# Context turned in two groups of 64 partitions in an adaLN cross-attention block (one core of Trainium2)

## The chip, the core and the metric

The kernel runs on one core of one Trainium2 chip. Its engines are TensorE (PE; PEld is its weight load), VectorE (DVE), ScalarE (ACT), GpSimd (POOL) and SyncE (SP), each with an instruction queue of its own that it works through in order. The metric is the device time of one launch in microseconds, lower being better. All numbers are float32 except a few bfloat16 helpers.

## The reference

One transformer block with modulation, for 16 batches of 224 tokens of width 512, 16 heads of 32, and a context of 750 rows per batch:

```python
x_norm = modulate(_ln(x), shift_a, scale_a)
q, k, v = split(x_norm @ W_qkv + b_qkv)             # self-attention
x = x + gate_a * (softmax(q k^T * scale) v @ W_proj + b_proj)
q_c = _ln(x) @ W_qc + b_qc                           # cross-attention
k_c, v_c = split(_ln(context) @ W_kvc + b_kvc)
x = x + (softmax(q_c k_c^T * scale) v_c @ W_cproj + b_cproj)
h = gelu(modulate(_ln(x), shift_m, scale_m) @ W_mlp1 + b_mlp1) @ W_mlp2 + b_mlp2
x = x + gate_m * h
```

The change touches only how `_ln(context)` is brought into the form that `k_c` and `v_c` are computed from.

## The kernel before

The kernel runs in three stages: self-attention (to about 727 us of the profiled execution), cross-attention (to about 2190 us), and the MLP. Nearly every instruction is issued through the `Ordered` helper (line 28 in the profile), so each engine's order is the program's order. Which tile waits for which is worked out from the tiles; a pool gives out its buffers in turn, and a tile waits until the readers of the tile that had the buffer before are done.

**Units.** Cross-attention runs over 64 units (b, g), batch b and group g of four heads (line 1093). A unit computes its scores in three parts n = 0, 1, 2, each of two chunks of 125 context rows; a part fills the four banks of `ps_s`, of which there is one set, so part n + 1 waits until part n has been read by `keep`: on VectorE into the running maximum `top`, and on ScalarE into the tile `pt`. After each part two slots of other work run: slots 0 and 1 after part 0, 2 and 3 after part 1, 4 and 5 after part 2. Between them lie the steps of the unit before: `subtract(0)` and `weights(0)` between slots 0 and 1, `subtract(1)` between slots 2 and 3, `weights(1)` after slot 3. `subtract` spreads the maxima on PE (`o<-ident,mc`) and adds them on VectorE; `weights` takes three exponentials on ScalarE and sums them on GpSimd. The unit ends with `maxima`, which turns `top` on PE into two banks. It turns rows 0 to 63 into one bank and rows 64 to 124 into the other, as two instructions of 64 and 61 rows. The next unit begins with the value products of the unit two before.

**The plan.** `at_slot(b, g, slot, f)` (lines 919 to 976) appends work to a slot; what is appended first runs first. What matters here, for batch b from 1 on, n = b + 1:

- slots 0 and 1 of every unit: `project_k` of the next unit's keys, halves 0 and 1 of the context (PE, then ScalarE empties the bank into `kt`);
- slots 2 and 4 of unit (b, 0): `project_v` of chunks 4 and 5 of batch b; slots 2 and 4 of (b, 2): of chunks 1 and 2 of batch n (PE, then ScalarE copies the bank into `vt`);
- slot 3 of (b, 0) and of (b, 2): the context of batch n is turned, half 0 and half 1, three chunks each (`turn_ctx`), and then the loads of batch b + 2 are issued on SP (`load_ctx`);
- slot 5 of these units: `project_q` (PE, then ScalarE into `qt`).

In batch 0, half 0 of the next batch is turned in slot 5 of (0, 0), the values of chunks 0 to 3 take other slots, and slot 0 of (0, 2) holds a product for a bias (`make_bcproj`). Before the first unit a prologue turns both halves of batch 0. Batch 15 turns nothing.

**PSUM.** All eight banks are in use: four for scores (`ps_s`), one for outputs (`ps_o`, line 235), and three in `ps_mm` (line 234: `name="at_mm", bufs=3`), from which `project_k`, `project_v`, `project_q`, `turn_ctx` and `maxima` take a bank each, and `maxima` two.

**Turning.** The context chunk `cx[b, c]` is a normalised tile of 125 rows on partitions and 512 columns. `turn_ctx(b, c)` turns its four blocks of 125 x 128 into one bank of 128 x 500, and ScalarE copies the bank into the half's tile `cxt` (128 partitions, 4 blocks, 375 rows). The chunk is the weight operand, a unit matrix of 125 x 125 is what streams.

## Time and profile before

| | |
|---|---|
| median of 3 runs | 2915.72 us (2912.17 to 2917.97) |
| the profiled execution: device time | 2912.48 us |
| its span, first to last instruction | 2910.7 us |
| mean granted TensorE clock | 0.993 |
| busy share of the span: PE, DVE, POOL, ACT | 97%, 66%, 43%, 38% |
| cross-attention, 742 to 2190 us: PE, DVE, POOL, ACT busy | 1416, 1132, 926, 829 us of 1448 |
| turns of `cx`: instructions, PE busy | 384, 46.7 us |
| copies of turned context on ScalarE: instructions, busy | 96, 49.3 us |

A line of a group has the source line, the engine, the operation, the tile written and those read, the shape and the count, then busy time and mean nanoseconds of one, then the engine's idle time before the group and what ended most of it. A line of a timeline has the start, the time from the first start to the last end of the merged instructions, engine, operation, and in brackets the idle time before. A line of the chain of waits has the start, the time that the chain spent there, and the engine and tile. One matrix product of float32 shows as two MATMUL records, a turn as one. PE's instructions overlap: a product or turn starts before the last one has ended, so the step from start to start is what a stream of them costs.

### The profile page before, as it was taken

How to read it: one execution, taken by the hardware profiler on the slowest of the kernel's cores; microseconds unless marked ns; L12 is line 12 of the kernel's file. 1: busy time of each engine (PE TensorE's matmuls, PEld its weight loads, DVE VectorE, ACT ScalarE, POOL GpSimd, SP SyncE). 2: the span in 40 equal slices, each digit the busy share in tenths (PEclk: the TensorE clock that was granted, in tenths of full speed). 3: DMA queues.
4: the chain of work that ended last, by engine and by line, in shares of the span. 5: the costliest groups of instructions: out<-in, count | busy, mean ns of one | idle time of the engine just before them, and what ended most of it. 6: DMA issues, size and time to landing. Idle time of an engine off the chain costs nothing.

```text
span 2910.7 us, 46976 instructions
## 1 busy us (share of the span) xinstructions
PE 2833.8 (97%) x19693; PEld 1809.3 (62%) x19693; DVE 1929.8 (66%) x2752; ACT 1119.6 (38%) x1402; POOL 1241.7 (43%) x1379
## 2 busy tenths in 40 slices
PE   8999999998999999999999999999978999999999
PEld 3444444444555565655655655666545888888888
DVE  4666776676478778787787787787785543444343
ACT  1222222221456655665565556656543112112211
POOL 1022222122357666676666666666654410221021
PEclk9999999999999999999999999999989999999999
DMA  6111110100100010100001100100013111110110
GB/s 191 59 33 33 32 33 10 60 11 29 52 32 24 22 35 24 35 32 21 29 25 34 35 24 23 34 25 24 22 44 107 55 37 37 44 57 29 46 44 29
DMA packets 55385, 114.44 MB, mean 39 GB/s; under 512 B 4309, under 2 KB 4373, under 8 KB 55173
## 3 DMA queue, kind: packets, MB, share of 16 engines
q1 hardware_dynamic: 54560, 110.58, 11.8%
q8 instruction: 155, 2.54, 0.4%
q10 hardware_dynamic: 612, 0.85, 0.1%
q14 instruction: 58, 0.47, 0.1%
HBM read 89.33 MB, written 22.09 MB: 38 GB/s over the span
## 4 chain that ended last, share of the span: by engine, by line
PE 79%; DVE 10%; ACT 5%; issue 4%; POOL 2%; DMA 1%; SPq 0%; POOLq 0%; ACTq 0%; DVEq 0%
PE mm L28 43%; PE a L28 10%; PE sc L28 10%; PE o L28 8%; PE b L28 5%; ACT pt L28 4%; DVE at L28 3%; PE c L28 3%; DVE top L28 2%; POOL acc L28 1%; DVE stats L28 1%; DVE m L28 1%; DVE mc L28 1%; ACT kt L28 1%; DMA gate<-gate_d 1%
## 5 line engine op out<-in xcount | busy, mean ns | idle before, releaser
L28 POOL TENSOR_TENSOR acc<-acc,pt 125x448 f32<-125x448 f32 x512 | 584.4, 1141 | 40.2
L28 ACT COPY pt<-sc 125x1792 f32<-125x1792 f32 x192 | 317.3, 1653 | 563.0 <-DVE top L28 509.9
L28 DVE TENSOR_TENSOR pt<-pt,o 125x896 f32<-125x896 f32 x384 | 394.2, 1081 | 87.0 <-PE o L28 84.6
L28 DVE TENSOR_TENSOR top<-top,sc 125x896 f32<-125x896 f32 x320 | 346.6, 1083 | 35.4 <-PE sc L28 28.7
L28 PE MATMUL mm<-wkvc,cxt 128*125 128x512 f32 x768 | 354.4, 604 | 6.9 <-ACT kt L28 6.9
L28 PE MATMUL mm<-cxt,wkvc 128*128 128x375 f32 x1024 | 353.3, 487 | 2.4 <-ACT cxt L28 2.4
L28 POOL TENSOR_TENSOR upd<-upd,gate 112x512 f32<-112x512 f32 (+1 forms) x60 | 78.9, 1315 | 631.7 <-DVE upd L28 627.1
L28 ACT ACTIVATE pt<-pt 125x896 f32<-125x896 f32 x384 | 338.3, 951 | 18.7 <-DVE pt L28 18.1
L28 POOL TENSOR_TENSOR acc<-pt 125x448 f32<-125x448 f32 x128 | 146.6, 1145 | 455.6 <-ACT pt L28 455.6
L28 PEld LDWEIGHTS mm<-cxt,wkvc 128*128 128x128 f32 x1024 | 184.7, 190 | 118.9 <-issue 15.4
L28 PEld LDWEIGHTS mm<-wkvc,cxt 128*125 128x125 f32 x768 | 136.4, 187 | 171.5 <-issue 153.3
L28 DVE RECIPROCAL at<-o 128x224 f32<-128x224 f32 x128 | 198.7, 1552 | 66.9 <-PE o L28 66.9
L28 ACT ACTIVATE pt<-sc 112x1792 f32<-112x1792 f32 x64 | 106.5, 1664 | 332.5 <-PE sc L28 327.9
L28 POOL TENSOR_TENSOR rstd<-mv,eps 112x2 f32<-112x2 f32 (+3 forms) x93 | 18.0, 193 | 468.7 <-DVE mv L28 468.7
L28 PE MATMUL sc<-qt,kt 32*125 32x224 f32 x3072 | 201.5, 376 | 13.9 <-ACT pt L28 13.3
L28 PE MATMUL mm<-xt,wqkv 128*128 128x448 f32 x512 | 208.6, 550 | 5.7 <-DVE xt L28 4.7
L28 DVE TENSOR_REDUCE m<-sc 112x8 f32<-112x1792 f32 x64 | 129.6, 2025 | 121.0 <-PE sc L28 121.0
L28 PEld LDWEIGHTS sc<-qt,kt 32*125 32x125 f32 x3072 | 132.9, 183 | 93.7 <-issue 33.4
L28 PE MATMUL o<-pt,vt 125*32 125x224 f32 x3072 | 158.6, 354 | 0.0
L28 PEld LDWEIGHTS mm<-xt,wqkv 128*128 128x128 f32 x512 | 92.0, 190 | 87.6 <-issue 80.4
L28 DVE TENSOR_REDUCE mc<-mm 112x8 f32<-112x512 f32 (+1 forms) x128 | 79.8, 666 | 98.4 <-PE mm L28 98.3
L28 ACT COPY mx<-a 128x512 f32<-128x512 f32 x26 | 15.2, 585 | 325.4 <-POOL upd L28 306.3
(187 smaller groups left out, 4687.2 us busy)
## 6 DMA issues: line engine op xcount, KB each, us to landing
cx<-in_ctx_dram SPq DMA_DIRECT2D x96, 250.0 KB
x<-in_x_dram SPq DMA_DIRECT2D x16, 448.0 KB
x_self<-x SPq DMA_DIRECT2D x16, 448.0 KB
x<-x_self SPq DMA_DIRECT2D x16, 448.0 KB
x_cross<-x SPq DMA_DIRECT2D x16, 448.0 KB
mx<-x_cross SPq DMA_DIRECT2D x28, 256.0 KB
w<-in_L_xcond_W_mlp_dram SPq DMA_DIRECT2D x7, 1024.0 KB
xr<-x_cross SPq DMA_DIRECT2D x28, 256.0 KB
```

The source lines that it names most:

```text
L28: return lambda *args, **kw: self.tc.keep_in_program_order(f(*args, **kw))
```

## The change

`turn_ctx` now takes a batch, a half and a list of chunks of that half. It takes two banks. Each block of a chunk is turned in two instructions, rows 0 to 63 (64 columns stream) into the first bank and rows 64 to 124 (61 columns) into the second. Chunks 0 and 1 of a half share a pair of banks; chunk 2 has a call, and a pair, of its own. ScalarE then makes one copy from each bank, in which the blocks and chunks of the bank are put in the order of `cxt`. For a half there are 24 turns where there were 12, four copies where there were three, and four banks taken where there were three.

In the plan, chunk 2 of a half goes to slot 1 of the unit, after `project_k` there, and chunks 0 and 1 to slot 3, where all three were. In batch 0, half 0 keeps slot 5 for both calls. In the prologue chunks 0 and 1 come first.

```diff
-        def turn_ctx(b, c):
-            if c % CH == 0:
-                cxt[b, c // CH] = cxt_pool.tile([P, KC, HS], F32, name="cxt")
-            ps = ps_mm.tile([P, 512], F32, name="mm")
-            for k in range(KC):
-                turn(ps[:, k * CP : (k + 1) * CP], cx[b, c][:, k * P : (k + 1) * P], ident[:CP, :CP])
-            lo = (c % CH) * CP
-            nc.scalar.copy(
-                cxt[b, c // CH][:, :, lo : lo + CP], ps[:, : KC * CP].rearrange("p (k t) -> p k t", k=KC)
-            )
+        def turn_ctx(b, hf, cs):
+
+            if (b, hf) not in cxt:
+                cxt[b, hf] = cxt_pool.tile([P, KC, HS], F32, name="cxt")
+            banks = [ps_mm.tile([P, 512], F32, name="mm") for _ in range(2)]
+            for j, c in enumerate(cs):
+                for k in range(KC):
+                    for i, (r, n) in enumerate(((0, RG), (RG, CP - RG))):
+                        lo = (j * KC + k) * n
+                        turn(
+                            banks[i][:, lo : lo + n], cx[b, hf * CH + c][r : r + n, k * P : (k + 1) * P],
+                            ident[r : r + n, r : r + n],
+                        )
+            j = len(cs)
+            dst = cxt[b, hf][:, :, cs[0] * CP : (cs[0] + j) * CP].rearrange("p k (j t) -> p k j t", j=j)
+            for i, (r, n) in enumerate(((0, RG), (RG, CP - RG))):
+                nc.scalar.copy(
+                    dst[:, :, :, r : r + n],
+                    banks[i][:, : j * KC * n].rearrange("p (j k t) -> p k j t", j=j, k=KC),
+                )
...
-                for c in range(CH):
-                    at_slot(b, 0, 3 if b else 5, lambda n=n, c=c: turn_ctx(n, c))
-                    at_slot(b, 2, 3, lambda n=n, c=c: turn_ctx(n, CH + c))
+                for cs, slot in (((2,), 1), ((0, 1), 3)):
+                    at_slot(b, 0, slot if b else 5, lambda n=n, cs=cs: turn_ctx(n, 0, cs))
+                    at_slot(b, 2, slot, lambda n=n, cs=cs: turn_ctx(n, 1, cs))
...
         for hf in range(2):
-            for c in range(hf * CH, (hf + 1) * CH):
-                turn_ctx(0, c)
+            for cs in ((0, 1), (2,)):
+                turn_ctx(0, hf, cs)
             load_ctx(1, hf)
             project_k(0, 0, hf)
```

## The prediction, made before the changed kernel ran

> **What bounds the kernel now.** I read the chain of waits first, for the engine that sets the end.

> ```profile
> PE 79%; DVE 10%; ACT 5%; issue 4%; POOL 2%; DMA 1%; SPq 0%; POOLq 0%; ACTq 0%; DVEq 0%
> ```

> TensorE sets it. Asked for the cross-attention stretch 742 to 2190 us alone, the busy times are PE 1416, DVE 1132, POOL 926, ACT 829 us of 1448. So time saved on PE counts, unless PE then waits. The groups by shape come next:

> ```profile
> L28 PE MATMUL mm<-ident,cx 125*128 125x125 f32 x384 | 46.7, 270 | 0.0
> L28 PE MATMUL mm<-ident,top 64*112 64x64 f32 x512 | 46.9, 224 | 1.7 <-DVE top L28 0.7
> L28 PE MATMUL mm<-ident,top 61*112 61x61 f32 x512 | 41.5, 221 | 1.5 <-ACT vt L28 1.1 <-ACT qt L28 0.2
> L28 ACT COPY cxt<-mm 128x500 f32<-128x500 f32 x96 | 49.3, 587 | 18.8 <-PE mm L28 17.8 <-POOL x L28 0.9
> ```

> The first row is what changes; the next two are turns already done in two groups (`maxima`), which give the price. I write (b, g) for a unit: batch b, head group g. The timeline of (4, 0) and (4, 2), the two units of batch 4 that turn context, shows one thing more: when ScalarE empties the bank of the second `kt` product.

> ```profile
> 1116.81 1.65 ACT L28 COPY pt<-sc 125x1792 f32<-125x1792 f32 x1 [7.17 <-DVE top L28]
> 1118.36 0.58 ACT L28 ACTIVATE kt<-mm,bcol 128x375 f32<-128x375 f32 x1
> 1118.82 2.63 ACT L28 ACTIVATE pt<-pt 125x896 f32<-125x896 f32 x3
> 1119.12 1.04 PE L28 MATMUL sc<-qt,kt 32*125 32x224 f32 x16
> 1120.08 3.70 PE L28 MATMUL mm<-wkvc,cxt 128*125 128x512 f32 x8
> 1121.34 0.57 ACT L28 ACTIVATE kt<-mm,bcol 128x375 f32<-128x375 f32 x1
> ...
> 1163.16 0.58 ACT L28 ACTIVATE kt<-mm,bcol 128x375 f32<-128x375 f32 x1
> 1163.31 1.04 PE L28 MATMUL sc<-qt,kt 32*125 32x224 f32 x16 [0.17 <-ACT pt L28]
> 1164.28 3.70 PE L28 MATMUL mm<-wkvc,cxt 128*125 128x512 f32 x8
> 1166.14 0.57 ACT L28 ACTIVATE kt<-mm,bcol 128x375 f32<-128x375 f32 x1
> ```

> In each unit the second `kt` product is emptied only after the first copy of the scores, the first `kt` and three exponentials: at 1121.91 and 1166.71. PE's value product (`mm<-wkvc,cxt`, slot 2) starts before that, at 1120.08 and 1164.28; it can, because its bank is another one.

> **The change, part by part.**

> *Turns on PE.* Out go 12 turns of 125 columns a half, which in (4, 0) take 1.45 us from first start to last end; less one turn's 0.27 that is 1.18 over 11 steps, 0.107 each. In come 24 turns, 12 pairs. The 16 paired turns of `top` at 1153.04, which nothing held, took 0.65 us; less one turn's 0.22, 0.43 for 8 pairs, about 56 ns a pair. The weights here have 128 columns and not 112. The nearest row with 128 columns and little to stream, the four `part` turns at 16.91 (0.42 us, less one of 0.21, three steps), gives at most 70 ns. So 8 turns take 0.22 to 0.28 and 16 take 0.44 to 0.56; I take 0.23 and 0.46, nearest to `top`. A change from full-height products to half-height turns costs about 0.09: the eight query products before `top` step by 0.19, and `top` follows the last by 0.28. From turns to scores I take 0.15 (`top` to `o` is 0.15), against 0.20 from the old turns.

> [...]

> *Slot 1, the third chunk.* Eight turns and two copies move to a place right after the second `kt` product, ahead of the second scores. In (4, 0) that is 0.23 + 0.15 = 0.38 us that PE did not have there: second scores at 1119.50. Queued behind are those scores, the value product, and with them everything on PE.

> *Banks.* The pool `at_mm` has three banks, given out in turn, so a tile waits for the one three before it. Old order in a unit: kt, kt, vt, cx, cx, cx, vt, qt, two of `maxima`. New: kt, kt, cxA, cxB, vt, cxC, cxD, vt, qt, two. So cxB now waits for the first `kt`, and the value product of slot 2 for the second. No order of giving out helps: at that moment second kt, cxA and cxB are all full. The turns and copies of slot 1 cannot be sooner.
> In (4, 0) cxB is free (1118.94) before its turns. The value product wants to start at 1120.08 + 0.38 = 1120.46, but its bank is empty at 1121.91, and PE follows ScalarE by about 0.05 (in (4, 2) the scores start at 1163.31 after the copy that ends at 1163.26): 1121.96, **1.88 us later** than before.
> In (4, 2) cxB waits until 1163.74 + 0.05; three more pairs and the change of height make the second scores 1164.14 instead of 1163.31 (0.83 later); the value product waits until 1166.71 + 0.05 = 1166.76, **2.48 us later**. What comes before that evacuation on ScalarE does not move: it hangs on VectorE's first maxima of the unit, and those on the unit's start.

> *Slot 3, the other two chunks.* PE: 12 old turns with the way to the scores, 1.28 + 0.20, against 0.09 + 0.46 + 0.15: about 0.7 us less. But the next thing is late. From the second subtraction's broadcasts (`o<-ident,mc`) VectorE runs three subtractions and two maxima without a pause, then ScalarE copies the scores and empties `vt`, and only then has the second bank of `maxima` its turn. The trace of before holds the experiment: (15, 0) has no turns in slot 3.

> ```profile
> 2107.64 0.44 PE o L28 x4
> ...
> 2109.11 2.08 DVE pt L28 x2
> 2111.19 1.01 DVE top L28
> ...
> 2113.41 1.65 ACT pt L28
> 2115.07 0.50 ACT vt L28
> ...
> 2115.61 0.65 PE mm L28 x15
> ```

> In this chain of waits of (15, 0) PE waits 1.13 us for `vt`. From the start of the broadcasts to the first values product it is 2107.48 to 2116.19, 8.71 us; in (4, 0), with all twelve turns, 1123.62 to 1132.32, 8.70; in (4, 2) 1167.81 to 1176.52, 8.71. **The turns in slot 3 are hidden, and halving them is worth nothing.** If that cover were gone they would be worth the 0.7.

> *Copies on ScalarE.* Three of 500 become two of 256 and 244 in slot 1 and two of 512 and 488 in slot 3. Three took 1.53; by `xt` (448 elements, 545 ns) and `qt` (224, 448 ns) the pairs take about 0.8 and 1.05. The first pair runs 1121.9 to 1122.7, ahead of the second scores' copy, which PE needs only by about 1126.7. The second pair ends 2.3 us after the broadcasts, the exponentials 2.65 later, and the third copy of the scores cannot start before 5.93 (1129.55 − 1123.62): 1.0 us of slack. Bounds: nothing, and, were each copy twice as long, 0.1 us a half. I take nothing. SP's context loads of slot 3 start with the turns, some 2 us later, for use a batch later.

> *Sum.* Batches 1 to 13: 13 × (1.88 + 2.48) = 56.7. Batch 14 has (14, 2) timed like (4, 0), the scores there not waiting: 2 × 1.88 = 3.8. In (0, 2) the bias product lies in slot 0; `kt` is emptied at 808.95 and the value product started at 807.65: 1.35. In (0, 0) all turns lie in slot 5, where cxC now waits for `qt` and the second bank of `maxima` for cxC's copy: about 0.6 (−0.5 to 1.5). Prologue: a fourth copy where three ended the wait (734.20 to 735.74): 0.25 (−1 to 1). Together 62.7 us. The profiled execution took 2912.48 us (span 2910.7), which gives 2975.2. The median of the runs is 3.2 above it; between the two I say **2977 us**.

> **The rivals.**
> 1. *The value product waits for nothing* (banks not in turn, or `kt` emptied sooner), but 8.70 holds. Then the units lose only what slot 1 adds: 14 × 0.38 + 13 × 0.83 + 2 × 0.38 and 1 elsewhere, 18 us in place of 62.7: 2932. For it: the old trace has no such wait. Against: three full banks.
> 2. *Faster: PE's shorter turns come through.* One mechanism: evacuation keeps ahead of PE in slots 1 to 5. It decides if the second `kt` is emptied 1.5 us sooner after the unit's start and the 8.70 shortens with PE. Then slot 1 costs 0.38 and slot 3 gives 0.7 in 29 halves, and in 13 of them a wait that is there now takes in 0.24 (first to second scores 6.90 us in (4, 2), 1156.41 to 1163.31, and 6.66 in (4, 0)): −29 × 0.32 − 13 × 0.24 = −12 us: 2902. For it: PE's 79% of the chain. Against: (15, 0).
> 3. *Copies slow.* If the reordered reads of 64 elements make a copy cost three times its row, the second pair takes 2.1 us longer, 1.1 beyond the slack, in 29 halves: +32, 3009. For it: no row has such a read. Against: `xt` and the old copies reorder nothing but stride too, at the price of plain ones.
> 4. *The two groups do not run side by side.* Then the pairs cost twice as much: 0.23 more in slot 1, inside the wait for `kt`, 0.46 in slot 3, inside the 1.1 that (15, 0) waits. In (b, 2) nothing more. Same time as the forecast, so it gets no share of its own.

> [...]

> **How the numbers follow.** The forecast has 0.83, rival 1 0.06, rival 2 0.05, rival 3 0.06. Its own unknowns (0.04 to 0.15 for PE to follow ScalarE in 29 waits, up to 3 us; the first batch and prologue, −3 to 3; copies, 0 to 3; runs against profile, ±3) make about −8 to +10. Toward the rivals I widen it to **2960 to 2992**, which leaves out the rivals, 0.17. No change means within 0.2%, 5.8 us, about what a measurement of this kernel can tell: 2910 to 2921, where no case lies: 0.01. Faster 0.05, slower 0.94.

> **What would show it.** In the new profile: turns of `cx` at some 56 to 62 ns a pair; in units (b, 0) and (b, 2) PE idle for about 1.5 and 1.6 us before the value product of slot 2, released by ACT `kt`; 8.70 unchanged; a batch of 93.8 us where it was 89.46 (first scores of (4, 0) at 1112.46, of (5, 0) at 1201.92). I am wrong if that wait is absent, or if the stretch of 8.70 shortens (rival 2) or grows (rival 3).

## The result and the profile after

The changed kernel takes **2986.47 us** (median of 4 runs, 2981.67 to 2988.08) against 2913.94 us (2912.1 to 2917.97): a ratio of 1.0243, 95% interval 1.0231 to 1.0255. It is slower by 72.5 us. The profiled execution took 2987.49 us, with a span of 2985.7 us and a mean granted clock of 0.989 (before: 2910.7 us and 0.993). The forecast was 2977 us, in a range of 2960 to 2992.

The chain of waits of the changed kernel, for the whole span:

```profile
PE 69%; DVE 13%; ACT 11%; issue 4%; POOL 2%; DMA 1%; SPq 0%; ACTq 0%; POOLq 0%; DVEq 0%
```

PE's share fell from 79% to 69%, while DVE rose from 10% to 13% and ACT from 5% to 11%: there is a new wait behind ScalarE. In the kernel before, the value products' group reads:

```profile
L28 PE MATMUL mm<-wkvc,cxt 128*125 128x512 f32 x768 | 354.4, 604 | 6.9 <-ACT kt L28 6.9
```

The groups by shape of the changed kernel say where the new wait is:

```profile
L28 PE MATMUL mm<-wkvc,cxt 128*125 128x512 f32 x768 | 361.2, 614 | 49.3 <-ACT kt L28 49.3
L28 PE MATMUL mm<-ident,top 61*112 61x61 f32 x512 | 41.5, 221 | 19.1 <-ACT vt L28 18.5 <-ACT cxt L28 0.6
L28 PE MATMUL mm<-ident,cx 61*128 61x61 f32 x384 | 37.2, 230 | 6.9 <-ACT kt L28 5.8 <-ACT cxt L28 1.1
L28 ACT COPY cxt<-mm 128x512 f32<-128x512 f32 x32 | 18.9, 590 | 33.6 <-PE mm L28 33.0 <-POOL x L28 0.6
L28 ACT COPY cxt<-mm 128x488 f32<-128x488 f32 x32 | 18.4, 575 | 0.0
L28 ACT COPY cxt<-mm 128x244 f32<-128x244 f32 x32 | 12.4, 388 | 0.0
L28 ACT COPY cxt<-mm 128x256 f32<-128x256 f32 x32 | 12.1, 378 | 0.0
```

PE's idle time ahead of the value products (first row) is 49.3 us, where it was 6.9, all of it ended by ScalarE's `kt`; the second bank of `maxima` (second row) waits 19.1 us, where it waited 1.5. The other rows are the new turns and the four sizes of copy. A busy time counts overlapping instructions, so the busy time of the turns says little; their steps do. In unit (4, 0) the pairs step by 61 to 64 ns from start to start, 110 ns for the first, and the two turns of a pair start within 0.01 us of each other.

The timeline of (4, 0), whose first scores start at 1136.78:

```profile
1142.68 0.58 ACT L28 ACTIVATE kt<-mm,bcol 128x375 f32<-128x375 f32 x1
...
1143.44 0.46 PE L28 MATMUL mm<-ident,cx 64*128 64x64 f32 x8
1143.83 1.04 PE L28 MATMUL sc<-qt,kt 32*125 32x224 f32 x16
1145.66 0.57 ACT L28 ACTIVATE kt<-mm,bcol 128x375 f32<-128x375 f32 x1
1146.12 0.64 ACT L28 COPY cxt<-mm 128x256 f32<-128x256 f32 x2
1146.29 3.70 PE L28 MATMUL mm<-wkvc,cxt 128*125 128x512 f32 x8 [1.43 <-ACT kt L28]
1149.82 0.59 PE L28 MATMUL o<-ident,mc 112*125 112x112 f32 x4
1150.34 0.71 PE L28 MATMUL mm<-ident,cx 64*128 64x64 f32 x16
1150.98 1.04 PE L28 MATMUL sc<-qt,kt 32*125 32x224 f32 x16
```

The value product starts at 1146.29, which is 9.51 us after the unit's first scores; before it was 1120.08 − 1112.46 = 7.62. It starts 0.06 us after the second `kt` is out of its bank (1145.66 + 0.57 = 1146.23), and the copies of the turned third chunk come behind that, so they are not what it waits for. The two subtractions' broadcasts and the third scores follow in step. The chain of waits of the same unit shows where the saving of slot 3 went:

```profile
1145.77 0.47 ACT kt L28
1146.24 0.04 issue
1146.29 3.70 PE mm L28 x8
...
1155.76 1.65 ACT pt L28
1157.41 0.50 ACT vt L28
1157.91 0.04 issue
1157.95 0.65 PE mm L28 x15
```

From the broadcasts at 1149.82 to the first values product at 1158.53 it is 8.71 us, as before, although the turns in between are shorter.

One thing was not forecast. In (1, 2) to (4, 2) the second broadcasts start 15.58 us after the first scores, from batch 5 on 13.89. Busy times of PE, PEld, DVE, ACT and POOL in three stretches around (1, 2), then the granted clock, DMA share and GB/s, and under them the value product of (1, 2):

```profile
903.30:906.70 3.40, 1.75 (x24) 1.30 (x25) 2.57 (x3) 3.40 (x7) 2.28 (x3) 1.00 0.13 39
906.70:910.20 3.50, 3.50 (x5) 1.32 (x4) 0.40 (x1) 1.80 (x2) 3.34 (x3) 0.51 0.09 35
910.20:913.60 3.40, 3.40 (x40) 2.23 (x38) 1.36 (x2) 1.31 (x3) 0.04 (x1) 1.00 0.01 2
...
906.38 5.39 PE L28 MATMUL mm<-wkvc,cxt 128*125 128x512 f32 x8 [1.55 <-ACT kt L28]
```

The new wait for `kt` lies in the first stretch: PE was busy for 1.75 of 3.40 us. In the next the granted clock is one half (0.50 from 906.75 to 910.16), and the value product takes 5.23 us to the broadcasts (906.38 to 911.61) where it took 3.53 in (4, 0): 1.70 us more. The trace has this stretch of 3.41 us in batches 1 to 4, 95.6 us apart, and then none until 2217.5 us.

### The profile page after: what moved, and what is told of

The parts are those of the page before. It is cut to its first block, busy times and chain, and to the rows that moved or that the text cites. A ratio compares the mean times of both kernels' runs of the same rounds, so it can differ in the third digit from the quotient of the medians.

```text
span 2985.7 us, 47772 instructions
## 1 busy us (share of the span) xinstructions
PE 2844.4 (95%) x20077; PEld 1806.2 (60%) x20077; DVE 1930.7 (65%) x2752; ACT 1123.6 (38%) x1434; POOL 1240.5 (42%) x1379
## 4 chain that ended last, share of the span: by engine, by line
PE 69%; DVE 13%; ACT 11%; issue 4%; POOL 2%; DMA 1%; SPq 0%; ACTq 0%; POOLq 0%; DVEq 0%
PE mm L28 36%; PE a L28 10%; ACT pt L28 8%; PE o L28 8%; PE sc L28 8%; PE b L28 5%; DVE top L28 4%; DVE at L28 3%; PE c L28 2%; ACT kt L28 1%; DVE pt L28 1%; POOL acc L28 1%; DVE stats L28 1%; DVE m L28 1%; DVE mc L28 1%
## 5 line engine op out<-in xcount | busy, mean ns | idle before, releaser
L28 POOL TENSOR_TENSOR acc<-acc,pt 125x448 f32<-125x448 f32 x512 | 583.5, 1140 | 40.1
L28 ACT COPY pt<-sc 125x1792 f32<-125x1792 f32 x192 | 317.3, 1653 | 574.3 <-DVE top L28 521.9
L28 DVE TENSOR_TENSOR pt<-pt,o 125x896 f32<-125x896 f32 x384 | 394.2, 1081 | 139.4 <-PE o L28 136.8
L28 PE MATMUL mm<-wkvc,cxt 128*125 128x512 f32 x768 | 361.2, 614 | 49.3 <-ACT kt L28 49.3
L28 DVE TENSOR_TENSOR top<-top,sc 125x896 f32<-125x896 f32 x320 | 346.5, 1083 | 51.9 <-PE sc L28 45.2
L28 POOL TENSOR_TENSOR acc<-pt 125x448 f32<-125x448 f32 x128 | 146.3, 1143 | 529.6 <-ACT pt L28 529.6
L28 PE MATMUL mm<-cxt,wkvc 128*128 128x375 f32 x1024 | 357.3, 491 | 1.3 <-ACT cxt L28 1.3
L28 ACT ACTIVATE pt<-pt 125x896 f32<-125x896 f32 x384 | 337.9, 948 | 20.5 <-DVE pt L28 19.9
L28 POOL TENSOR_TENSOR upd<-upd,gate 112x512 f32<-112x512 f32 (+1 forms) x60 | 78.9, 1315 | 632.1 <-DVE upd L28 627.5
L28 PEld LDWEIGHTS mm<-wkvc,cxt 128*125 128x125 f32 x768 | 138.8, 190 | 220.4 <-issue 149.8
L28 PEld LDWEIGHTS mm<-cxt,wkvc 128*128 128x128 f32 x1024 | 186.8, 192 | 119.8 <-issue 18.8
L28 DVE RECIPROCAL at<-o 128x224 f32<-128x224 f32 x128 | 198.7, 1552 | 68.2 <-PE o L28 68.2
L28 ACT ACTIVATE pt<-sc 112x1792 f32<-112x1792 f32 x64 | 106.5, 1663 | 332.2 <-PE sc L28 332.2
L28 PE MATMUL mm<-xt,wqkv 128*128 128x448 f32 x512 | 208.6, 550 | 5.7 <-DVE xt L28 4.7
L28 POOL TENSOR_TENSOR rstd<-mv,eps 112x2 f32<-112x2 f32 (+3 forms) x93 | 18.0, 193 | 470.7 <-DVE mv L28 470.7
L28 PE MATMUL sc<-qt,kt 32*125 32x224 f32 x3072 | 201.9, 377 | 11.7 <-ACT pt L28 11.1
L28 DVE TENSOR_REDUCE m<-sc 112x8 f32<-112x1792 f32 x64 | 129.6, 2025 | 121.1 <-PE sc L28 121.1
L28 PEld LDWEIGHTS sc<-qt,kt 32*125 32x125 f32 x3072 | 133.4, 184 | 75.0 <-issue 29.4
L28 PE MATMUL o<-pt,vt 125*32 125x224 f32 x3072 | 158.6, 355 | 0.0
L28 PEld LDWEIGHTS mm<-xt,wqkv 128*128 128x128 f32 x512 | 92.0, 190 | 87.6 <-issue 80.4
L28 DVE TENSOR_REDUCE mc<-mm 112x8 f32<-112x512 f32 (+1 forms) x128 | 79.8, 665 | 99.0 <-PE mm L28 99.0
L28 ACT COPY mx<-a 128x512 f32<-128x512 f32 x26 | 15.2, 585 | 325.4 <-POOL upd L28 306.3
```

Source lines behind the costliest of these rows:

```text
L28: return lambda *args, **kw: self.tc.keep_in_program_order(f(*args, **kw))
```

## The experiments

The first four were compared with runs of the kernel before at 2915.29 us, the next two at 2916.66, the last four at 2916.14.

### Banks, halving and new places

**Both calls of a half in slot 3.** The changed kernel, but no turns in slot 1:

```diff
-                for cs, slot in (((2,), 1), ((0, 1), 3)):
+                for cs, slot in (((2,), 3), ((0, 1), 3)):
```

> The changed kernel, but chunk 2 goes back to slot 3, ahead of chunks 0 and 1: paired turns, old places. Bank theory (the cost comes from taking two banks in slot 1, between the second kt product and the value product): the value product's bank is free again, units (b, 0) and (b, 2) are as long as in the kernel before, since the stretch of 8.70 us from the second subtraction's broadcasts to the first values product hides the turns whether they are whole or halved: 2913 to 2921 us. Rival (the paired turns or their copies cost the time themselves): stays near 2975 to 2986. Rival (halved turns are worth their 0.7 us a half on PE): about 2893.

2921.13 us, ratio 1.0019 (1.0009 to 1.0028). The value product is back at 7.63 us after the first scores, and a batch takes 89.60 us (before 89.46). Nothing of the halving arrives. But the run doesn't show that the cover alone took it: with four banks wanted in slot 3 the turns stop for a bank, and from the second broadcasts to the third scores it is now 2.08 us (1130.40 to 1132.48) where whole turns took 1.80, and from the broadcasts to the first values product 8.77. The cover needed a test of its own, below.

**Whole turns in the new places.** The kernel before, with three banks a half, chunk 2 in slot 1:

```diff
-            if c % CH == 0:
+            if (b, c // CH) not in cxt:
...
+                for c, slot in ((2, 1), (0, 3), (1, 3)):
+                    at_slot(b, 0, slot if b else 5, lambda n=n, c=c: turn_ctx(n, c))
+                    at_slot(b, 2, slot, lambda n=n, c=c: turn_ctx(n, CH + c))
```

> The kernel before, with whole turns and one bank a chunk, but chunk 2 in slot 1 as in the changed kernel. Bank theory: the value product now waits for the first kt, emptied long before, so only the longer slot 1 costs: 0.43 us in (b, 0) (0.31 + 3 x 0.107 + 0.20 in place of 0.41) and 0.19 in (b, 2), where 0.24 of waiting is used up; 14 x 0.43 + 13 x 0.19 + 0.9, some 9 us: 2920 to 2926. Rival (the move to slot 1 is what costs, by the work it puts ahead of the second scores and the copies ahead of their evacuation): 2970 or more.

2924.45 us, ratio 1.0031 (1.0019 to 1.0043). The value product starts at 8.05 us, without a wait: one bank in slot 1 is not enough to make it follow `kt`. A batch takes 90.09 us, and the second bank of `maxima` starts 0.65 us after the first where it was 0.22: the 0.43 us of turns taken out of slot 3 come back there.

**Banks only.** The kernel before, which also takes two banks in slot 1 of (b, 0) and (b, 2) and puts one small turn of a constant in each; two small copies go to a tile that nobody uses. The context is turned as before.

```diff
+        def two_banks():
+            banks = [ps_mm.tile([P, 512], F32, name="mm") for _ in range(2)]
+            for i, (r, n) in enumerate(((0, RG), (RG, CP - RG))):
+                turn(banks[i][:, :n], ones[r : r + n, :], ident[r : r + n, r : r + n])
+            for i, n in enumerate((RG, CP - RG)):
+                nc.scalar.copy(spare[:, i, :n], banks[i][:, :n])
```

> The kernel before with its whole turns in slot 3, and in slot 1 of the same units two banks taken for nothing: one small turn of a constant into each (64 and 61 columns) and a small copy of each on ScalarE. Bank theory: nothing of the changed kernel but its banks, and yet its time: the value product of slot 2 starts 1.88 us later in (b, 0) and 2.48 later in (b, 2), and the total is 2970 to 2990. Rival (halved turns, reordered copies or their number cost the time): 2914 plus some 0.3 us in each of 29 units, 2923.

3002.84 us, ratio 1.0306 (1.0288 to 1.0323). Two banks with next to no work in them give value products at 9.51 us in (b, 0) and 10.35 in (b, 2), the same as in the changed kernel. That is the mechanism by itself. It costs more than expected, because here the clock falls to 0.50 in twelve batches, (2, 2) to (13, 2), and a batch takes 95.55 us; all value products together take 374.7 us, where they took 354.4 in the kernel before. One of these in the windows of this run, columns as above:

```profile
1567.00:1570.30 3.30, 1.50 (x18) 1.08 (x19) 2.66 (x3) 3.20 (x7) 2.27 (x2) 1.00 0.00 0
1570.30:1573.70 3.40, 3.40 (x5) 1.35 (x5) 0.28 (x1) 1.65 (x1) 3.19 (x3) 0.50 0.00 0
```

### The evacuation

**The second `kt` ahead of the exponentials.** The changed kernel, and as a control the kernel before, with slot 1 run ahead of `weights(0)`, so that ScalarE empties the second `kt` first:

```diff
-                if n == 0 and prev:
-                    prev.weights(0)
-                run(plan, (b, g, 2 * n + 1))
+                if n == 0:
+                    run(plan, (b, g, 1))
+                    if prev:
+                        prev.weights(0)
+                else:
+                    run(plan, (b, g, 2 * n + 1))
```

> The changed kernel with slot 1 run ahead of the three exponentials of weights(0), so that ScalarE empties the second kt before them and not after. Bank theory: the bank is empty by about 7.3 us after the unit's first scores, before the value product wants it (8.0); what is left is 0.38 us in (b, 0), and in (b, 2) 0.85, where the pair's second bank still waits for the first kt: 13 x 1.23 + 0.76 + the prologue's 2, 2930 to 2938. Rival (the wait is for something else, or the exponentials take its place on the path): 2975 or more.

> The kernel before with slot 1 run ahead of weights(0): the control for the same reordering of the changed kernel. If the order of the exponentials and the second kt does nothing by itself, 2910 to 2918 us; if it has a gain or a loss of its own, that is to be taken off the changed kernel with that order.

The changed kernel falls to 2927.65 us, ratio 1.0041 (1.0026 to 1.0056), 2.4 us below the range that was expected, which had nothing for the order itself; the control takes 2909.96 us, 0.9975 (0.9965 to 0.9984). In the first the timeline of (4, 0) reads:

```profile
1127.40 0.46 PE L28 MATMUL mm<-ident,cx 64*128 64x64 f32 x8
1127.51 0.58 ACT L28 ACTIVATE kt<-mm,bcol 128x375 f32<-128x375 f32 x1 [0.28 <-PE mm L28]
1127.80 1.04 PE L28 MATMUL sc<-qt,kt 32*125 32x224 f32 x16
1127.98 0.63 ACT L28 COPY cxt<-mm 128x256 f32<-128x256 f32 x2
1128.49 2.65 ACT L28 ACTIVATE pt<-pt 125x896 f32<-125x896 f32 x3
1128.76 3.70 PE L28 MATMUL mm<-wkvc,cxt 128*125 128x512 f32 x8
```

`kt` is out at 1128.09, the value product follows the scores with no wait, and the time is 59 us below the changed kernel's, where the order alone is worth 6.7 in the control. A batch takes 90.02 us, in the control 88.73. The 1.29 between them is what slot 1 costs without the late bank: the second scores come at 7.05 instead of 6.66 us in (b, 0), and at 7.77 instead of 6.89 in (b, 2), where the turns still wait for the first `kt`.

**The wait filled.** The changed kernel, with six products of constants into the free output bank ahead of the value product in slot 2 of (b, 0) and (b, 2). Their result is not used.

```diff
+        def fill():
+            o = ps_o.tile([P, 512], F32, name="o")
+            for _ in range(6):
+                mm(o[:, :P], ones, ident, start=True, stop=True)
...
+            if b and n < B:
+                at_slot(b, 0, 2, fill)
...
+                at_slot(b, 2, 2, fill)
```

> The changed kernel with six products of two constant tiles (128 x 128 by 128, about 1.3 us) into the free output bank ahead of the value product of slot 2 in units (b, 0) and (b, 2), b from 1 to 14 and (0, 2): PE works while it would wait for ScalarE. Their results are used by nothing. Clock theory (the waits let the granted clock fall to a half for 3.4 us at a time, in (1, 2) to (4, 2), which is 1.70 us each beyond the forecast): the value products of these four units take 3.5 us as in the others, and the kernel is some 5 to 10 us faster than the changed one, 2975 to 2982. Rival (those value products are slow for another reason): no faster than the changed kernel, 2982 to 2990.

2983.75 us, ratio 1.0232 (1.0215 to 1.0249): above the 2975 to 2982 expected, and not to be told from the changed kernel's 1.0243. The time alone would speak for the rival; the trace does not. Around (1, 2) of this run the columns as above read:

```profile
906.40:909.80 3.40, 3.38 (x35) 2.59 (x32) 2.56 (x3) 3.13 (x6) 2.69 (x3) 1.00 0.18 63
909.80:913.20 3.40, 3.40 (x13) 1.62 (x13) 0.00 (x0) 2.06 (x2) 2.98 (x3) 1.00 0.05 17
```

PE is busy through the wait, the clock stays at 1.00 in the stretch that follows, and no stretch of half clock is left between 850 and 2200 us. All value products together take 354.3 us, where it was 361.2 in the changed kernel and 354.4 in the kernel before; batches 1 to 4 take 93.85 us like the others, 4 × 1.70 = 6.8 us less. The units also lie some 2.7 us later in this execution, and in the trace of the changed kernel the stretches start whole steps of 3.41 us apart (last section), so the move alone could have ended them. The six products took 1.60 us in (1, 2), and by an estimate from the records of this trace PE would without them have been busy for 1.43 to 1.57 us in one such step in seven of the batches; with them it was 2.97 to 3.10. In the banks-only run PE busy for 1.50 us (1567.00 to 1570.30) came ahead of half clock, and in the changed kernel 1.80 us (903.34 to 906.75). By that estimate the filling kept the clock up. In this profiled execution 2.3 us of that are lost again before the first unit (at 746.30 instead of 744.05), and 0.4 in batch 0.

### The cover in slot 3

**`vt` ahead of the copy of the third scores.** The changed kernel, in which ScalarE copies slot 4's `vt` before the third scores in (b, 0) and (b, 2); PE's order stays. The same edit went into the control with the early `kt`.

```diff
-            def keep(self, n, st):
+            def keep(self, n, st, key=None):
...
+                if key:
+                    run(plan, key)
                 nc.scalar.copy(pt, st[:CP, :, : 2 * N])
...
-                cur.keep(n, st)
+                early = n == 2 and g % 2 == 0 and b + g > 0 and b < B - 1
+                cur.keep(n, st, (b, g, 4) if early else None)
```

> The changed kernel, with one thing on ScalarE put another way round: in (b, 0) and (b, 2), slot 4's copy of vt is issued ahead of the copy of the third scores, not behind it. PE's order is untouched. My theory of the cover: the 0.7 us that the shorter turns save in slot 3 are there, but are given back as 0.86 us of wait before the second bank of maxima, whose bank slot 4's vt holds until ScalarE has copied the third scores. With vt emptied in the 1.0 us of slack before that copy the wait goes and the stretch from the second subtraction's broadcasts to the last turn of maxima falls from 8.56 to 7.70 us: 29 units x 0.86 = 25 us, about 2961 us (2952 to 2967; the half-clock stretches of the first batches may move or go). Rival: the stretch is held by VectorE's maxima and the copy of the scores, and putting vt first only makes that copy late: 2984 to 2992 us and 8.56 unchanged. The wait for kt in slot 2 stays in both.

> The kernel before, whole turns, with slot 1 ahead of the exponentials (as in the control of the second call) and vt ahead of the third scores' copy. The wait before the second bank of maxima is only 0.22 us there, so by my theory the second part gains 29 x 0.22 = 6.4 us on top of the control's 2910: about 2904 us (2898 to 2908), the stretch 8.34 us. Rival as for the run before: 2910, 8.56 unchanged.

The first takes 2958.04 us, ratio 1.0143 (1.0129 to 1.0157): 28.4 us less than the changed kernel. A batch takes 92.13 us where it was 93.83, and the stretches of half clock of batches 1 to 4 are absent (6.8 us: the value products take 354.4 us together, not 361.2). Its timeline of (4, 0), second broadcasts at 1140.16:

```profile
1146.03 0.59 ACT L28 COPY vt<-mm 125x512 f32<-125x512 f32 x1 [1.01 <-PE mm L28]
1146.51 1.66 ACT L28 COPY pt<-sc 125x1792 f32<-125x1792 f32 x1
1147.43 0.52 PEld L28 LDWEIGHTS mm<-ident,top 64*112 64x112 f32 x16 [0.28 <-issue]
1147.43 0.66 PE L28 MATMUL mm<-ident,top 64*112 64x64 f32 x16
1148.02 2.48 PE L28 MATMUL o<-pt,vt 125*32 125x224 f32 x48
```

All 16 turns of `maxima` run through, and from the broadcasts to the first values product it is 7.86 us, not 8.71. From the broadcasts to the last turn it is 7.71 instead of 8.56: the 0.64 that shorter turns save, and the 0.22 that was lost before the change too. The copy of the scores starts 0.4 us later (6.35 after the broadcasts instead of 5.94) and nothing waits for it. The second run, whole turns with both orders, takes 2901.04 us, 0.9948 (0.9935 to 0.9960): with only 0.22 us of wait to remove, 8.56 becomes 8.35, and a batch goes from 88.73 to 88.33 us.

### Versions that take the gain

Both have the two orders of the run just told. In the first the paired third chunk is turned right behind the unit's first scores:

```diff
-                for cs, slot in (((2,), 1), ((0, 1), 3)):
+                for cs, slot in (((2,), -1), ((0, 1), 3)):
...
+                if n == 0:
+                    run(plan, (b, g, -1))
```

In the second only chunks 0 and 1 are turned in pairs, and all three in slot 3, the third whole in one bank; the prologue turns whole:

```diff
-                for cs, slot in (((2,), 1), ((0, 1), 3)):
+                for cs, slot in (((0, 1), 3), ((2,), 3)):
...
+            groups = ((0, RG), (RG, CP - RG)) if j > 1 else ((0, CP),)
+            banks = [ps_mm.tile([P, 512], F32, name="mm") for _ in groups]
```

> The changed kernel's paired turns with both orders of the run before, and the third chunk turned right behind the unit's first scores, ahead of the first kt product, so that its two banks are emptied before ScalarE's first copy of the scores and no product waits for a bank. By my theory each half then costs PE 0.38 us in its new place and gains 0.64 (turns of slot 3) against whole turns in the same orders: 28 x 0.26 = 7 us less than the run before, about 2897 us (2890 to 2903), second scores at 7.05 us in (b, 0) and (b, 2), value product right behind. Rival: the early copies or the bank order bring another wait, and the time is that of the run before or more.

> Both orders again, nothing in a new slot: in slot 3 the first two chunks are turned in pairs of 64 partitions into two banks, the third whole into one bank, three banks as in the kernel before; the context before the first unit is turned whole. By the steps seen so far PE needs 0.09 + 8 x 0.061 + 4 x 0.107 + 0.20 = about 1.2 us in place of 1.48 for a half: 28 x 0.28 = 8 us less than whole turns in these orders, about 2896 us (2888 to 2902). Rival: the stretch is then bound by something else than PE, and the time is 2904.

They take 2898.71 us, ratio 0.9938 (0.9925 to 0.9950), and 2899.17, 0.9941 (0.9928 to 0.9955). Both are faster than the kernel before and the changed one, by 0.6% and 3%; against whole turns in the same orders (0.9948) the intervals overlap. The traces tell the three apart: a batch takes 87.87 and 88.20 us against 88.33. The first in (4, 0), first scores at 1112.31:

```profile
1113.28 0.46 PE L28 MATMUL mm<-ident,cx 64*128 64x64 f32 x8
...
1113.77 0.64 ACT L28 COPY cxt<-mm 128x256 f32<-128x256 f32 x2 [4.28 <-PE mm L28]
...
1119.36 1.04 PE L28 MATMUL sc<-qt,kt 32*125 32x224 f32 x16
1119.47 0.57 ACT L28 ACTIVATE kt<-mm,bcol 128x375 f32<-128x375 f32 x1 [0.70 <-PE mm L28]
...
1120.33 3.70 PE L28 MATMUL mm<-wkvc,cxt 128*125 128x512 f32 x8
```

The two banks are emptied in ScalarE's pause before its first copy of the scores, second scores come at 7.05 us, and the value product follows without a wait: as expected. In (4, 2) they come at 7.34 and not 7.05; the copies start 4.19 us after the first scores there, not 1.46, and why was not followed up. Of the 7 us, 6.4 arrive in 14 batches; the prologue, batch 0 and what comes after the first scores of (15, 0) are together 2.9 us longer. In the second the third chunk makes the saving small: from the second broadcasts to the third scores 1.74 us against 1.80. My sum had taken 1.48 for the whole turns there, but they take 1.37 (1123.46 to 1124.83 in the trace of the whole turns), and the new ones 1.31 with the change of height, not 1.2, so 0.28 a half was too much.

## Why the prediction was right, and where it was short

| us against the kernel before, in the profiled executions | forecast | measured |
|---|---|---|
| first scores of (0, 0) | 0.25 | 2.07 |
| batch 0 | 1.95 | 4.10 |
| batches 1 to 13 | 56.7 | 63.5 |
| batch 14 | 3.8 | 3.8 |
| after the first scores of (15, 0) | 0 | 1.5 |
| sum | 62.7 | 75.0 |

*The banks: right.* The value product was to come 1.88 us later in (b, 0) and 2.48 in (b, 2); 9.51 − 7.62 = 1.89, and 10.35 − (1164.28 − 1156.41) = 2.48. A batch was to take 93.8 us and takes 93.83 from batch 5 on. That the banks do it, not the turns or the copies, is shown from two sides: two banks with nothing useful in them bring the same start, and an earlier evacuation takes it away.

*The turns: right.* 56 to 70 ns a pair was the bound, 61 to 64 the result, and the two turns of a pair start within 0.01 us of each other: the two groups run side by side.

*The saving of slot 3 is hidden: right, and by the cover named.* 8.71 us stayed, and with `vt` emptied first it shrank to 7.86. The 0.7 were 0.64 (1.80 to 1.16 us from the second broadcasts to the third scores). The sum had counted twelve steps and the way to the scores for the old turns, 1.48 us; from the first of them to the scores it is 1.37 in the old trace (1124.04 to 1125.42), eleven steps and the way.

*The copies: right.* The pairs were to take 0.8 and 1.05 us and took 0.64 and 1.06. Reordered reads of 64 elements cost nothing extra here (590 ns for 512 elements, 587 for the old 500).

*Rivals.* The first (no wait, 2932) describes the run with the early `kt` (2927.65) and not the change. What was said for it, that the old trace has no such wait, was a misreading. In every (b, 3) from batch 0 to 14 two turns of `x` in slot 2 take two banks between the second `kt` product and the value product of slot 3, and in (4, 3), whose first scores start at 1179.31, the kernel before shows:

```profile
1188.82 3.70 PE L28 MATMUL mm<-wkvc,cxt 128*125 128x512 f32 x8 [0.46 <-ACT kt L28]
```

That is 9.51 us after the first scores, as in the changed (b, 0): the mechanism and its time could be read there before the change was made.

The second (the gain comes through) needed two conditions, the early `kt` and a shorter 8.70; with both made, and the third chunk moved, PE's shorter turns do come through, at 0.46 us a batch. The third (slow copies) fell.

*What was short: the clock.* Four times 1.70 us in batches 1 to 4, 6.8 of the 12.3 us missing (75.0 − 62.7), are stretches of half clock, and the new waits bring them about: in the run that fills the waits they are gone. The term that was too small is 13 × (1.88 + 2.48): it took PE's products after a wait at the price they had without one. The prediction's list of unknowns has no clock in it, so that the time still lay in the range is partly luck. The banks-only run starts its value products at the same times and met twelve such stretches; eight more here would have cost 13.6 us and brought the time to some 3000 us, outside the range. In the prologue the term of 0.25 was 0.50 for the fourth copy and the bank, which is the start of the second `kt` product (736.29 against 735.79), and 1.57 because that product met half clock (0.50 from 736.09 to 739.50), as the changed kernel's timeline shows:

```profile
736.29 4.36 PE L28 MATMUL mm<-cxt,wkvc 128*128 128x375 f32 x8 [0.67 <-ACT cxt L28]
```

It took 2.79 us before. That this is the change's own price is not shown. The control with the early `kt` turns whole chunks in the prologue, and there the same product met half clock too (0.50 from 740.00 to 743.40):

```profile
739.67 4.48 PE L28 MATMUL mm<-cxt,wkvc 128*128 128x375 f32 x8 [1.76 <-ACT cxt L28]
```

In batch 0, (0, 0) is 0.61 us longer, as forecast, and (0, 1) 0.39, which was not in the sum. In (0, 2) scores and `kt` product took 1.87 and 4.65 us at half clock (0.50 from 797.52 to 804.35) in place of 1.04 and 2.79, partly inside a wait that was there before: the first broadcasts come 9.73 us after the first scores, not 7.94, 1.79 later. From them to the value product it is 1.35 us longer, as forecast. That the 1.79 are the change's own is not shown either. The 1.5 us after the first scores of (15, 0) were not followed up; in the control that part is 1.7 us longer than before, without the change.

## What to carry to other kernels

When a tile asks for more buffers of a small pool, count which tile each later request now follows, and when that one is emptied on its engine: an extra bank cost 1.9 to 2.5 us here where the work in it cost 0.4 to 0.8. Look for the same order of requests elsewhere in the old trace: its wait may already be there to be read. A saving on an engine only shows if the next gate in line moves too, so look for the step whose wait would grow, and move that evacuation ahead of the long copy in front of it. A wait of 1.55 us on PE cost more than itself here: the clock behind it was 0.50, and the value product took 5.23 us in place of 3.53.

## What the hardware did unexpectedly

In the changed kernel a wait of 1.55 us (904.83 to 906.38) lay within the step ahead of the first of the four. The step ahead of each of them had PE busy for 1.80 to 1.86 us, summed from the records of its products and turns; but about the same before (5, 2), 1.86 us from 1285.63, was followed by full clock. Summed in the same way over the cross-attention of both traces (to 2190 and to about 2265 us), the steps at full clock with PE busy for 1.34 us or less, nine of them, were all followed by half clock, and those with 1.87 or more all by full clock. In between there were nine, from 1.80 to 1.86 us, four followed by half clock and five by full; what decides there is open. Outside that stage it was not so: in the kernel before, a step with 1.41 us (from 2903.18) was followed by full clock. In the `vt`-first run, with the same wait for `kt` (49.5 us in all) and a batch of 27 steps (92.13 us), the wait keeps its place in its step too, but none of the four stretches comes; why is not shown.
